# The closing LayerNorm of the last two graphs, block by block on VectorE with separate stores

## Chip, cores and metric

The kernel runs on one core of a Trainium2 chip. The metric is device time in microseconds (us) of one execution, as the median of several. The core's engines work side by side, each through its own instructions in order: TensorE (PE in the profile; PEld is its weight loads), VectorE (DVE), ScalarE (ACT), GpSimd (POOL) and SyncE (SP), which issues the DMA transfers. They wait for each other through semaphores.

## The reference

64 graphs of 256 nodes with 256 features each pass four graph-attention layers. After each layer a residual is added and the rows are normalized without gain or bias:

```python
x = _layernorm(x + _L0_gnn_ref(x, adj, ...), axis=-1)   # 4 heads, projections, own norm
x = _layernorm(x + _L1_gnn_ref(x, adj, ...), axis=-1)   # 8 heads, then a GELU MLP of 1024
x = _layernorm(x + _L2_gnn_ref(x, adj, ...), axis=-1)   # additive attention scores
x = _layernorm(x + _L3_gnn_ref(x, adj, ...), axis=-1)   # scores (x * a_k) @ x.T by edge type
return x
```

`_layernorm` is `(x - m) / sqrt(v + 1e-5)` over the 256 features of a row. For layer 3 the weights are a softmax over the neighbours of a node; only the normalization that follows layer 3, the one that makes the output, is touched here.

## The kernel before

A graph is two blocks (q = 0 and 1) of 128 nodes; a tile `[128, 2, 256]` holds both blocks of a graph, nodes on the 128 partitions. Each graph's work is cut into seven generators named a, u, z, b, w, c and o (`thread_a` to `thread_o`), and each `yield` in them ends a step. Many graphs are in flight together. The order of the steps is written out by hand: `FIRST` lists the steps of the start, `PLACES` gives every step of the middle a due time relative to its graph, and `LAST` lists the steps of the closing stretch, as pairs of a thread's letter and a graph (counted from graph 48 in base 36, so `oe` is a step of `thread_o` of graph 62 and `of` one of graph 63). A small wrapper, `InOrder` (L466), ties each engine's instructions to this order; that is why nearly all rows of the profile carry its line L475, and why groups are told apart by tiles.

`thread_o` (L991) is layer 1's second MLP product, layer 2 and layer 3. Its end goes like this. `values_of` (L974) takes the blocks in the order 1, 0. For each it makes two matmuls into a PSUM tile `pm` (softmax weights times values, and a column with the sum of weights); VectorE takes the reciprocal `r` of that sum and computes `y = pm * r + x` with `scalar_tensor_tensor`, whose accumulator output gives the row sum `sums`. `renormed` (L961) then calls `moments` (L636), in which ScalarE squares the centred rows of both blocks (`xn<-y,sums`, with an accumulator output `sq`), and GpSimd works on two columns at once, one for each block: `ve` from `sq`, `rstd = ve ** -0.5`, and in two instructions `nm = -mean * rstd`. `scaled` (L655) has ScalarE write `xn = y * rstd + nm`, one instruction a block, and SyncE stores both blocks of the graph with one DMA of 256 KB (`out<-xn`). Where no `sums` are handed over, `renormed` uses `stats` (L614) instead, in which VectorE's `bn_stats` and `bn_aggr` make mean and variance `mv`; and `scaled` without `nm` uses VectorE's `tensor_scalar`.

Behind the last step of the plan stand some checks of the input (L1155 to L1171): maxima and sums in `tops`, comparisons `good`, their minimum `all_good`, a matmul over the partitions and the comparison `flag`. They are issued straight to the engines, not through `InOrder`, so that they may be placed anywhere that their data allow. All five engines then load `flag` (L1180) and branch on it (L1181) past a slow general version of the kernel (`any_input`), which the inputs measured here don't need. The rows of L1204 are the closing waits and the barrier of all engines.

Of the kernel before, what the change touches and what calls it, by code (L numbers as in the profile page):

```python
# [8 lines left out]
F32 = mybir.dt.float32  # L9
# [4 lines left out]
ALU = mybir.AluOpType  # L14
AX = mybir.AxisListType

P = 128
N = 256
D = 256
NC = D // P  # L20
G = 2
QB = N // P
TB = G * QB
T = G * N
W = D + 4
DFF = 1024
NF = DFF // P
EPS = 1e-5
# [12 lines left out]
PSR = True  # L41
SQ = True
WARM = 2
XQ = True
DIRECT = {0: ('x', 'z', 'o', 'yT'), 63: ('yT', 'n2', 'n3', 'o')}
BUFS = {'t': 7, 'q': 3, 'k': 1, 'v': 3, 'y': 4, 'z': 4, 'xb': 4, 'both': 2, 'xn': 6, 'mask': 9, 'e': 7, 'x0': 3, 'turned': 2, 'blk': 4, 'oT': 3, 'zs': 1, 'rr': 2, 'xT': 1, 'qT': 1, 'kT': 1, 'adj': 2, 'adjb': 1, 'adjT': 1, 'hT': 2, 'ea': 3}
# [403 lines left out]
def usual_input(ctx: ExitStack, tc: tile.TileContext, a: dict, out: bass.AP, flag: bass.AP):  # L450

    nc = tc.nc
    B = a["x"].shape[0]
# [4 lines left out]
    act = ctx.enter_context(tc.tile_pool(name="act", bufs=1))  # L458
    small = ctx.enter_context(tc.tile_pool(name="small", bufs=8))
# [25 lines left out]
    PE, DVE, ACT, POOL, SP = (InOrder(e) for e in (nc.tensor, nc.vector, nc.scalar, nc.gpsimd, nc.sync))  # L485
    matmul, transpose = PE.matmul, PE.transpose

    def new(pool, shape, dtype, name, bufs=None, tag=None):
        tag = tag or name
        if bufs is None:  # L490
            bufs = BUFS.get(tag)
        t = pool.tile(shape, dtype, name=name, tag=tag, **({} if bufs is None else dict(bufs=bufs)))
        return t
# [3 lines left out]
    warm = new(ps_s, [P, 2, QB * N], F32, "ps", 2)  # L497
    for _ in range(WARM):
        matmul(warm[:, 0, :].rearrange("p (k j) -> p k j", k=4), ones, ones.unsqueeze(1).to_broadcast([P, 4, P]), start=True, stop=True)
    ident = const.tile([P, P], F32, name="ident")  # L500
    make_identity(nc, ident)
    mhalf = const.tile([P, 2 * TB], F32, name="mhalf")
# [11 lines left out]
    r_3 = const.tile([P, B, QB], F32, name="r_3")  # L514
# [6 lines left out]
    def load_x(g):  # L521
        turned = None
        if FX and "x" not in DIRECT.get(g, ()):
            turned = new(io, [P, NC, N // 32, 32], F32, "turned")
            parts = a["x"][g].rearrange("(t i) (c k j) -> k i c t j", i=32, c=NC, j=32)
            for k in range(P // 32):
                if XQ:
                    SP.dma_start(turned[32 * k:32 * k + 32], parts[k])
                for c in range(0 if XQ else NC):
                    SP.dma_start(turned[32 * k:32 * k + 32, c], parts[k, :, c])  # L530
# [83 lines left out]
    def stats(src, twice=False, centre=False):  # L614

        k = 2 if twice else 1
        st = new(small, [P, QB, 6], F32, "st", 8)
        mv = new(small, [P, QB, 2], F32, "mv", 12)
        for q in range(QB):
            DVE.bn_stats(st[:, q, :], src[:, q, 0:D])  # L620
        for q in range(QB):
            DVE.bn_aggr(mv[:, q, :], st[:, q, :])
        ve = new(small, [P, k, QB], F32, f"ve{k}", 8)
        POOL.tensor_scalar(ve[:, 0], mv[:, :, 1], EPS, None, ALU.add)
        if twice:
            POOL.tensor_scalar(ve[:, 1], mv[:, :, 1], 1.0 + EPS, EPS * EPS, ALU.mult, ALU.add)
        rstd = new(small, [P, k, QB], F32, f"rstd{k}", 12)
        POOL.tensor_tensor(rstd, ve, mhalf[:, 0:k * QB].rearrange("p (k t) -> p k t", k=k), ALU.pow)
        nm = None
        if centre:  # L630
            nm = new(small, [P, QB], F32, "nm", 12)
            POOL.tensor_tensor(nm, mv[:, :, 0], rstd[:, k - 1], ALU.mult)
            POOL.tensor_scalar(nm, nm, -1.0, None, ALU.mult)
        return mv, rstd, nm, ve
# [326 lines left out]
    def renormed(y, sums=None):  # L961
        if sums is None:
            mv, rstd, nm, _ = stats(y, centre=SCN)
        xn = new(act, [P, QB, W], F32, "xn")
        POOL.memset(xn[:, :, D:D + 1], 1.0)
        if sums is not None:
            rstd, nm, _ = moments(y, sums, xn)
            mv = None
        yield
        scaled(xn, y, mv, rstd[:, 0], nm)  # L970
        yield
        return xn

    def values_of(e, v, one, x, rs):  # L974
        y = None
        for q in (1, 0):
            po = new(ps_m, [P, one + 1], F32, "pm", 4)
            for kc in range(QB):
                matmul(po, e(kc, q), v[:, kc, 0:one + 1], start=kc == 0, stop=kc == QB - 1)
            yield  # L980
            if y is None:
                y = new(act, [P, QB, D], F32, "y")
                sums = new(small, [P, QB], F32, "sums", 8) if SQ else None
            r = rs[:, q:q + 1]
            DVE.reciprocal(r, po[:, one:one + 1])
            DVE.scalar_tensor_tensor(y[:, q, :], po[:, 0:D], r, x[:, q, 0:D], ALU.mult, ALU.add,
                                     **(dict(accum_out=sums[:, q:q + 1]) if SQ else {}))
            yield
        return y, sums

    def thread_o(g, s):  # L991
        mask = s["mask"]
        hT = s["hT"]
        pm = new(ps_m, [P, QB, D], F32, "pm", 4)
        for q in range(QB):
            for c in range(NF):
                matmul(pm[:, q, :], hT[:, c, q * P:(q + 1) * P], w2[:, c, :], start=c == 0, stop=c == NF - 1)
            yield
        y = s["both"]
        DVE.tensor_tensor(y, pm, y, ALU.add)  # L1000
        yield
        x = yield from renormed(y)

        xT = yield from flipped(x, not FN2, "n2", g)
        yield
        wh = new(act, [P, QB, W], F32, "v")
        pms = []
        for q in range(QB):
            pm = new(ps_m, [P, D + 3], F32, "pm", 4)
            for c in range(NC):  # L1010
                matmul(pm, xT[:, q, c, :], wx[:, c, :], start=c == 0, stop=c == NC - 1)
            pms.append(pm)
        yield
        POOL.memset(wh[:, :, D + 3:D + 4], 1.0)
        for q in range(QB):
            ACT.copy(wh[:, q, 0:D + 3], pms[q])
        ex = new(small, [P, QB, 3], F32, "ex", 4)
        ACT.activation(ex, wh[:, :, D:D + 3], AF.Exp)
        yield
        pt = new(ps_m, [P, N], F32, "pm", 4)  # L1020
        for q in range(QB):
            transpose(pt[:, q * P:(q + 1) * P], ex[:, q, 0:1].to_broadcast([P, P]), ident)
        yield
        e2 = new(act, [P, QB, N], F32, "q")
        for kc in range(QB):
            DVE.tensor_scalar(e2[:, kc, :], pt, ex[:, kc, 1:2], ex[:, kc, 2:3], ALU.mult, ALU.max)
        DVE.tensor_tensor(e2.rearrange("p k q -> p (k q)"), e2.rearrange("p k q -> p (k q)"), mask, ALU.mult)
        yield
        y, sums = yield from values_of(lambda kc, q: e2[:, kc, q * P:(q + 1) * P], wh, D + 3, x, new(small, [P, QB], F32, "r", 8))
        x = yield from renormed(y, sums)  # L1030

        xT = yield from flipped(x, not FN3, "n3", g)
        yield
        xa = new(act, [P, QB, NC, P], F32, "t")
        for c in range(NC):
            ACT.activation(xa[:, :, c, :], xT[:, :, c, :], AF.Identity, scale=a0[:, c:c + 1])
        yield
        ps = new(ps_m, [P, N + P], F32, "pm", 4)
        for kc in range(QB):
            for c in range(NC):  # L1040
                if kc == 0:
                    matmul(ps[:, 0:N].rearrange("p (q j) -> p q j", q=QB), xT[:, 0, c, :], xa[:, :, c, :],
                           start=c == 0, stop=c == NC - 1)
                else:
                    matmul(ps[:, N:N + P], xT[:, 1, c, :], xa[:, 1, c, :], start=c == 0, stop=c == NC - 1)
        yield
        e = new(act, [P, QB * N], F32, "q")
        low = new(act, [P, N + P], F32, "k")
        most = e[:, 0:N + P]
        ACT.activation(most, ps, AF.Exp, bias=shift)  # L1050
        ACT.activation(low, ps, AF.Exp, bias=shift, scale=SLOPE)
        yield
        DVE.tensor_tensor(most, most, low, ALU.max)
        for to, of in ((slice(0, N), slice(0, N)), (slice(N, N + P), slice(N + P, 2 * N))):
            DVE.tensor_tensor(e[:, to], e[:, to], mask[:, of], ALU.mult)
        yield
        pt = new(ps_m, [P, P], F32, "pm", 4)
        transpose(pt, e[:, P:N], ident)
        yield
        ACT.copy(e[:, N + P:2 * N], pt)  # L1060
        yield
        at = ((0, P), (N + P, N))
        y, sums = yield from values_of(lambda kc, q: e[:, at[kc][q]:at[kc][q] + P], x, D, x, r_3[:, g])
        x = yield from renormed(y, sums)
        SP.dma_start(out[g].rearrange("(q p) d -> p q d", p=P), x[:, :, 0:D])
        yield

    def loading():
# [68 lines left out]
    def threads_of(g):  # L1137
        s = {}
        return {"a": thread_a(g, s), "u": thread_u(g, s), "z": thread_z(g, s), "b": thread_b(g, s), "w": thread_w(g, s),
                "c": thread_c(g, s), "o": thread_o(g, s)}  # L1140
# [67 lines left out]
```

## Time and profile before

| what | value |
|---|---|
| median of 3 runs | 2371.16 us (2369.64, 2371.16, 2371.6) |
| profiled execution, its own time | 2374.09 us |
| its span | 2372.3 us |
| TensorE busy | 2338.2 us, 99% |
| VectorE busy | 1924.6 us, 81% |
| ScalarE busy | 1819.8 us, 77% |
| GpSimd busy | 686.9 us, 29% |
| stores of the output | 64 DMAs of 256 KB |
| end of TensorE's last attention product | 2361.43 us |
| end of ScalarE's last scaling | 2366.27 us |
| issue of the last store | 2366.30 us |

The span is the stretch from the first to the last recorded instruction; the execution's own time includes what lies around it. Lines of a timeline give the start in us from the span's start, the length in us, the engine, the source line, the operation, its tiles (out<-in) and how many instructions are merged; a bracket names the idle time before and what ended it. A "q" behind an engine's name stands for its sequencer: waits, branches and DMA issues.

### The profile page before, as it was taken

What the parts mean: (1) busy time and instruction counts of PE and PEld (TensorE: products, weight loads), DVE (VectorE), ACT (ScalarE), POOL (GpSimd) and SP (SyncE); (2) the same over time, 40 slices, a digit from 0 to 9 for tenths busy, and PEclk for the clock granted to TensorE, in tenths of its full rate; (3) what the DMA queues carried; (4) which work ended last, traced back from release to release, by engine and by line L of the source; (5) the groups of instructions that cost most, each with busy time, mean ns of one, the idle gap of its engine ahead of it and who ended that gap; (6) DMA issues with size and microseconds to landing.
All of it is one profiled execution on the core that took longest, in us unless ns stands there. A gap on an engine that the chain in (4) does not pass through costs nothing.

```text
span 2372.3 us, 50135 instructions
## 1 busy us (share of the span) xinstructions
PE 2338.2 (99%) x16124; PEld 1882.1 (79%) x16124; DVE 1924.6 (81%) x6175; ACT 1819.8 (77%) x3976; POOL 686.9 (29%) x1742
## 2 busy tenths in 40 slices
PE   8999999999999999999999999999999999999997
PEld 5677788788788788788788887887887887877786
DVE  5898888888878878878888888888788788778764
ACT  5677877778787788788777777787877887777766
POOL 1122323322332332223223223223323232323232
PEclk9999999999999999999999999999999999999999
DMA  5455555555555555555555555555545545455442
GB/s 129 103 113 118 109 117 112 110 117 116 110 120 111 115 120 112 117 116 110 123 112 107 121 113 111 118 112 112 121 111 116 119 110 120 103 109 116 90 86 68
DMA packets 1088884, 265.08 MB, mean 112 GB/s; under 512 B 859364, under 2 KB 1088232, under 8 KB 1088616
## 3 DMA queue, kind: packets, MB, share of 16 engines
q1 hardware_dynamic: 1088136, 261.42, 51.3%
q8 instruction: 130, 2.13, 0.4%
q14 instruction: 138, 1.13, 0.2%
q10 hardware_dynamic: 416, 0.39, 0.1%
q0 software_dynamic: 64, 0.00, 0.0%
HBM read 153.37 MB, written 99.88 MB: 107 GB/s over the span
## 4 chain that ended last, share of the span: by engine, by line
PE 90%; DMA 3%; ACT 2%; DVE 2%; SPq 2%; issue 1%; POOL 1%; DVEq 0%; ACTq 0%; POOLq 0%
PE pm L475 80%; PE ps L475 10%; SPq L475 2%; DMA blk<-rows 1%; ACT xn L475 1%; DMA rows<-z 1%; DMA turned<-in_x 0%; ACT e L475 0%; DMA adj<-in_adj 0%; DVE y L475 0%; ACT z L475 0%; POOL rstd L475 0%; DMA rr<-lines 0%; DVE e L475 0%; DVE xT L475 0%
## 5 line engine op out<-in xcount | busy, mean ns | idle before, releaser
L475 DVE SCALAR_TENSOR_TENSOR e<-e,mask 128x256 f32<-128x256 f32 x1024 | 368.8, 420 | 210.9 <-ACT e L475 210.8
L475 PE MATMUL pm<-t,L_gnn_W 128*128 128x256 f32 x2048 | 459.7, 382 | 0.4 <-ACT oT L475 0.4
L475 PE MATMUL pm<-L_gnn_W,hT 128*128 128x256 f32 (+1 forms) x2064 | 455.0, 380 | 0.1
L475 PEld LDWEIGHTS pm<-t,L_gnn_W 128*128 128x128 f32 x2048 | 384.5, 190 | 67.4 <-issue 16.1
L475 PEld LDWEIGHTS pm<-L_gnn_W,hT 128*128 128x128 f32 (+1 forms) x2064 | 389.2, 189 | 54.6 <-issue 1.7
L475 ACT ACTIVATE e<-ps 128x1024 f32<-128x1024 f32 x384 | 381.1, 1018 | 51.4 <-PE ps L475 50.7
L475 POOL TENSOR_TENSOR rstd<-ve,mhalf 128x2 f32<-128x2 f32 (+1 forms) x384 | 314.4, 819 | 32.0
L475 POOL TENSOR_SCALAR ve<-sq 128x2 f32<-128x2 f32 x256 | 75.4, 294 | 798.1 <-ACT xn L475 526.8
L475 POOL TENSOR_SCALAR ve<-mv 128x2 f32<-128x2 f32 x192 | 48.1, 251 | 784.5 <-DVE rz L475 462.1
L475 DVE STREAM_TRANSPOSE t<-blk 128x512 f32<-128x512 f32 x313 | 219.6, 704 | 16.7 <-DMA blk<-rows 16.1
L475 ACT ACTIVATE hT<-pm,b 128x256 f32<-128x256 f32 x512 | 201.2, 474 | 17.3 <-PE pm L475 16.5
L475 ACT ACT_TABLE_LOAD x127 | 162.9, 1283 | 2.4 <-PEq L1194 0.7
L475 DVE TENSOR_TENSOR e<-e,mask 128x1024 f32<-128x1024 f32 x128 | 150.9, 1218 | 11.6 <-ACT e L475 11.5
L475 PE MATMUL ps<-t 32*128 32x256 f32 x2048 | 151.1, 404 | 5.2 <-ACT t L475 4.1
L475 ACT ACTIVATE xn<-y,nm,rstd 128x256 f32<-128x256 f32 x256 | 138.5, 593 | 11.0 <-POOL nm L475 9.0
L475 ACT ACTIVATE xn<-y,sums 128x256 f32<-128x256 f32 x256 | 126.6, 497 | 18.2 <-DVE y L475 18.0
L475 PEld LDWEIGHTS ps<-t 32*128 32x128 f32 x2048 | 95.5, 186 | 56.5 <-ACT oT L475 19.7
L475 ACT ACTIVATE few_out<-few 128x8 f32<-128x8 f32 x64 | 13.3, 208 | 162.2 <-DVE few L475 162.1
L475 POOL TENSOR_SCALAR nm<-nm 128x2 f32<-128x2 f32 x320 | 128.9, 403 | 28.0
L475 PE MATMUL pm<-xn,q 128*128 128x257 f32 x512 | 130.9, 381 | 3.5 <-ACT q L475 3.4
L475 DVE SCALAR_TENSOR_TENSOR y<-pm,r,xn 128x256 f32<-128x256 f32 x256 | 123.9, 484 | 9.6
L475 PE MATMUL pm<-e,v 128*32 128x256 f32 x2048 | 124.0, 383 | 5.0 <-DVE e L475 4.6
(149 smaller groups left out, 4646.0 us busy)
## 6 DMA issues: line engine op xcount, KB each, us to landing
blk<-rows SPq DMA_DIRECT2D x1252, 64.0 KB, 2.4
rows<-xn SPq DMA_DIRECT2D x252, 128.0 KB, 2.1
x<-in_x SPq DMA_DIRECT2D x64, 256.0 KB, 3.3
adj<-in_adj SPq DMA_DIRECT2D x64, 256.0 KB, 3.6
rr<-lines SPq DMA_DIRECT2D x128, 128.0 KB, 3.7
out<-xn SPq DMA_DIRECT2D x64, 256.0 KB, 2.5
turned<-in_x SPq DMA_DIRECT2D x252, 64.0 KB, 2.6
rows<-z SPq DMA_DIRECT2D x126, 128.0 KB, 1.9
```

The costliest lines, as they stand in the source:

```text
L475: ins = call(*args, **kw)
```

## The change

A new constant `LATE = 2` selects the last two graphs, 62 and 63. For all others nothing is changed. For these two:

- `values_of` gets a function that it calls as soon as a block's `y` is there, and no longer accumulates `sums`.
- That function takes `bn_stats` and `bn_aggr` of the one block on VectorE, and on GpSimd `ve` and `rstd` of one column.
- After both blocks, VectorE scales them (block 1, then block 0) with `tensor_scalar`, `(y - mean) * rstd`, and each block is stored by a DMA of its own, 128 KB.
- ScalarE's squares and scalings, GpSimd's two `nm` instructions and the memset of a column of ones in `xn` are gone for these graphs. The number of steps of `thread_o` stays, and `LAST` is unchanged.

```diff
+LATE = 2
...
-    def values_of(e, v, one, x, rs):
+    def values_of(e, v, one, x, rs, after=None):
...
-                sums = new(small, [P, QB], F32, "sums", 8) if SQ else None
+                sums = new(small, [P, QB], F32, "sums", 8) if SQ and after is None else None
...
-                                     **(dict(accum_out=sums[:, q:q + 1]) if SQ else {}))
+                                     **({} if sums is None else dict(accum_out=sums[:, q:q + 1])))
+            if after is not None:
+                after(y, q)
             yield
...
-        y, sums = yield from values_of(lambda kc, q: e[:, at[kc][q]:at[kc][q] + P], x, D, x, r_3[:, g])
-        x = yield from renormed(y, sums)
-        SP.dma_start(out[g].rearrange("(q p) d -> p q d", p=P), x[:, :, 0:D])
+        block = lambda kc, q: e[:, at[kc][q]:at[kc][q] + P]
+        if g < B - LATE:
+            y, sums = yield from values_of(block, x, D, x, r_3[:, g])
+            x = yield from renormed(y, sums)
+            SP.dma_start(out[g].rearrange("(q p) d -> p q d", p=P), x[:, :, 0:D])
+            yield
+            return
+        known = {}
+
+        def block_done(y, q):
+            st = new(small, [P, QB, 6], F32, "st", 8)
+            mv = new(small, [P, QB, 2], F32, "mv", 12)
+            DVE.bn_stats(st[:, q, :], y[:, q, 0:D])
+            DVE.bn_aggr(mv[:, q, :], st[:, q, :])
+            ve = new(small, [P, 1, QB], F32, "ve1", 8)
+            POOL.tensor_scalar(ve[:, 0, q:q + 1], mv[:, q, 1:2], EPS, None, ALU.add)
+            rstd = new(small, [P, 1, QB], F32, "rstd1", 12)
+            POOL.tensor_tensor(rstd[:, 0, q:q + 1], ve[:, 0, q:q + 1], mhalf[:, q:q + 1], ALU.pow)
+            known[q] = mv, rstd
+
+        y, _ = yield from values_of(block, x, D, x, r_3[:, g], block_done)
+        xn = new(act, [P, QB, W], F32, "xn")
+        for q in (1, 0):
+            mv, rstd = known[q]
+            DVE.tensor_scalar(xn[:, q, 0:D], y[:, q, :], mv[:, q, 0:1], rstd[:, 0, q:q + 1], ALU.subtract, ALU.mult)
+            SP.dma_start(out[g, q * P:(q + 1) * P, :], xn[:, q, 0:D])
+            yield
         yield
```

## The prediction

> **What bounds the kernel now.** I read the page first, then its chain of work that ended last, then the last 15 us instruction by instruction, because the diff touches only graphs 62 and 63.
>
> ```profile
> span 2372.3 us, 50135 instructions
> ...
> PE 2338.2 (99%) x16124; PEld 1882.1 (79%) x16124; DVE 1924.6 (81%) x6175; ACT 1819.8 (77%) x3976; POOL 686.9 (29%) x1742
> ...
> PE 90%; DMA 3%; ACT 2%; DVE 2%; SPq 2%; issue 1%; POOL 1%; DVEq 0%; ACTq 0%; POOLq 0%
> ```
>
> The reader sees TensorE (PE) busy 99% of the span and carrying 90% of the chain. In the built order of the changed program TensorE's instructions are the same in number and order, and the other engines differ only from the closing steps of graphs 61 to 63 on. So everything before about 2359 us keeps its time, and only the tail can move. Its timeline (start, length, engine, operation):
>
> ```profile
> 2361.68 0.48 DVE L475 SCALAR_TENSOR_TENSOR y<-pm,r,xn 128x256 f32<-128x256 f32 x1
> ...
> 2362.48 0.14 DVE L1165 TENSOR_SCALAR good<-tops 128x1 f32<-128x1 f32 x1
> ...
> 2363.20 3.07 ACT L475 ACTIVATE xn<-y,nm,rstd 128x256 f32<-128x256 f32 x6
> ...
> 2363.42 0.14 DVE L1171 TENSOR_SCALAR flag<-pm 1x1 int32<-1x1 f32 x1 [0.48 <-PE pm L1170]
> ...
> 2364.30 3.02 SPq L475 DMA_DIRECT2D out<-xn  x3
> ```
>
> The last attention sum is ready on VectorE (DVE) at 2362.16, ScalarE (ACT) scales six blocks until 2366.27, and SyncE issues the last store at 2366.30. Yet the span ends at 2372.3: 6 us follow. The other string of work is the flag: VectorE has it at 2363.56, and then every engine branches on it (L1181) and meets in a barrier (L1204). The rows of those two lines (duration min/median/max in ns, first and last start):
>
> ```profile
> L1181 SPq EVENT_SEMAPHORE  x8: 17/17/17, 2368.5 to 2370.3; - x8
> L1181 PEldq COMPARE_BRANCH  x1: 4229/4229/4229, 2364.2 to 2364.2; - x1
> ...
> L1181 ACTq COMPARE_BRANCH  x1: 45/45/45, 2366.0 to 2366.0; - x1
> ```
>
> ```profile
> L1204 ACTq EVENT_SEMAPHORE  x2: 17/17/17, 2371.4 to 2372.3; - x2
> L1204 DVEq EVENT_SEMAPHORE  x2: 21/21/21, 2371.5 to 2372.3; - x2
> ...
> L1204 PEldq EVENT_SEMAPHORE  x2: 51/51/51, 2371.9 to 2372.3; - x2
> ```
>
> TensorE's branch takes 4.23 us where ScalarE's takes 0.05. In the stretch 2364.5 to 2365.5 the DMA view has one 16 KB packet on instruction queue q8 at 10.5% of 16 engines over 1 us, which is 1.7 us; from 2368.5 to 2370 there is another at 4.0% over 1.5 us, 1.0 us. I read them as TensorE's code loads. The barrier opens for ScalarE and VectorE at 2371.4 to 2371.5, for TensorE only at 2371.9, and all leave at 2372.3. So two strings end together: stores landed (SyncE's eight waits, done 2370.3), and **flag to TensorE**: 2363.56 + 8.76 = 2372.3.
>
> **The change part by part.** Call the blocks X1, X0 (graph 62) and Y1, Y0 (graph 63).
>
> *Removed:* on ScalarE eight ACTIVATEs (four squares, four scalings, 0.5 to 0.6 each) and four accumulator reads of 0.19. They end the store string now; what is late next decides.
>
> *VectorE.* The accumulator read (0.08) goes. Each block now is: weighted sum 0.48, bn_stats 0.40 (row mean of st<-y), bn_aggr 0.17, the next reciprocal 0.16, gaps of 0.04 between dependent ones (2334.82 + 0.17 to 2335.02 is one), less 0.05 overlap: 1.28 a block. From the first sum at 2359.27 the blocks start at 2359.27, 2360.55, 2361.83, 2363.11; TensorE, done at 2361.43, is no longer what they wait for. The last bn_aggr ends at 2364.42, with the two L1162/L1163 reductions in its gaps. That is 2.3 later than the last sum ends now.
>
> *GpSimd (POOL)* works in order: X1, X0, then all of graph 61's norm, then Y1, Y0. Rows between 2358 and 2366: ve 0.19, rstd 0.71, nm 0.20 and 0.22, gaps 0.08. The one-column rstd is not in the trace: two columns cost 0.71 and the four-column row averages 1.06, which would give 0.57 on that slope; above I bound it by 0.71. X0 can start at 2361.76 (0.08 behind its bn_aggr) and ends 2362.6 to 2362.75. Graph 61, which starts its ve at 2360.21 today, then needs 0.17 + 1.57 and ends at 2364.35 to 2364.5; its two scalings and its store go 2.5 us later, beside the rest. Y1 and Y0 need 0.80 to 0.99 each: Y0's rstd is there at 2365.95 to 2366.4. The gain of dropping ScalarE's squares is given back in this queue.
>
> *VectorE again.* The four scalings stand in the order X1, Y1, X0, Y0, so X1 starts only behind the last bn_aggr and X0 waits behind Y1 for Y1's rstd, though its own is 2.6 us old. The last scaling starts at 2366.03 to 2366.45. A 128x256 tensor_scalar from SBUF to SBUF is not in the trace: the copy hT<-bv of that size takes 0.28, q<-pm,ex 0.54 from PSUM; I take 0.4. It ends at 2366.3 to 2367.0 against ScalarE's 2366.27. So the store string gains nothing: -0.0 to +0.7 at the last issue.
>
> *Stores:* 256 KB for each graph as before, in two halves; SyncE issues two more (0.37 each, spread over 2 us, hidden behind the waits for scalings). A lone 256 KB store landed after 2.2, the last three after 3.6 to 4.2; a half bounded by 2.2 and 3.6 lands at 2368.6 to 2370.6, against 2369.9 now.
>
> *The flag moves behind the norm.* The checks L1165 to L1171 are not held by the hand-written order; in the built program good, all_good and flag stand on VectorE after the four scalings. Today they take 1.09 us (2362.48 to 2363.56) while VectorE is idle. Now they start 0.07 before the last scaling ends: flag at 2367.35 to 2367.97, **3.8 to 4.4 later**, 4.05 with middle values. Behind it wait TensorE's and VectorE's branches. TensorE's code loads lie on that path; the first took 1.7 us beside three 256 KB stores, the second 1.0 alone. Most stores will have landed by the new first load (about 2369.2), so I take 0.5 off (bounds 0 and 0.7). Sum: 4.05 - 0.5 = **+3.5 us** (bounds +3.1 to +4.4). The span becomes 2375.8.
>
> *A rule that bears on it.* The Trainium skill, "Runtime: NRT & Kernel Launch", section Instruction fetch mechanics, says that a taken branch whose target is not in the loaded window waits for a DMA fetch of the page; TensorE's 4.23 us and the q8 packet agree. "Advanced Engine Details and Errata", section Control Flow Timing, gives a compare-and-branch about 108 ns; ScalarE's 45 ns fits that order of size, TensorE's row does not, and the row decides. By 108 ns the flag string would have 4 us to spare and the sum would be that of the third rival.
>
> The profiled execution took 2374.09, 1.8 beyond its span; the median of the three runs is 2371.16, 2.9 below it. I add the difference to the median: 2371.16 + 3.5 = **2374.7 us**, +0.15%. About 0.2% (4.74 us, beyond 2375.9 or below 2366.4) is what a measurement of this kernel can tell from no change.
>
> **The rivals.**
>
> 1. *GpSimd is held up by VectorE, slower by more than 0.2%.* Over the whole run GpSimd's rows are longer than in the quiet tail: nm 0.40 against 0.20, rstd 0.77 against 0.71, ve 0.25 to 0.29 against 0.19. Today VectorE is mostly idle while GpSimd works in the tail; after the change it runs bn_stats and scalings beside it. At these means the four ve/rstd pairs and two nm after X1 grow by 4 x 0.16 + 2 x 0.19 = 1.0, on top of the upper 4.4, less 0.5: +4.9, 2376.1. It decides from 1.2 us that Y0's rstd comes later than my middle 2366.2. For it: those means. Against it: beside weighted sums in the tail (2361.68 to 2362.16) the rows kept their 0.71 and 0.22.
>
> 2. *TensorE's second load is not waited for.* Then the late 2371.9 is only a slow poll, and the end follows from TensorE's arrival (2368.5 now): 4.05 - 0.5 puts it at 2372.0, SyncE's last waits and the barrier add 1.6: span 2373.6, +1.3, 2372.5. Against it: the packet at 2368.5 to 2370 and the 0.5 us that TensorE alone is late.
>
> 3. *The change does what its words say for the stores, and the flag stays hidden.* TensorE's branch would have to be short, so that only the last landing counts: 2368.6 to 2370.6 instead of 2369.9, middle -0.5: 2370.7. Against it: the 4.23 us row.
>
> **How the numbers follow.** Forecast 58% (own range 2373.5 to 2376.2, its bounds and 0.5 to 1 us for the spread of the runs, 2369.64 to 2371.6; about a tenth of it lies beyond 2375.9). Rival 1 18%, all counted as slower. Rival 2 12%, rival 3 12%, of which 3 points for a gain beyond 0.2% that I can't derive. Slower 0.06 + 0.18 = 0.24, faster 0.03, same 0.73. The range 2371.5 to 2376.6 takes in the forecast, rival 2 and most of rival 1 and leaves out rival 3.
>
> **What would show it.** Right: TensorE's instructions end near 2361.4 as now; Y0's rstd ends near 2366.2 behind a GpSimd queue without idle gaps from 2361.8; the last VectorE scaling ends near 2366.6; flag near 2367.6; TensorE's branch 3.5 to 4.2 long; its barrier row near 2375.4 and later than the other engines'. Wrong: a flag before the scalings, a TensorE branch under 1 us, a barrier that opens for all engines at once, or GpSimd pairs over 1.1 us. If anything before 2359 us moves, the reading that only the tail is touched is wrong.

## The result and the profile after

The kernel after takes **2376.73 us** (median of 11 runs, 2373.96 to 2379.72), the kernel before in 11 runs 2371.16 us (2369.64 to 2374.53). The ratio is 1.0019 with a 95% interval of 1.0011 to 1.0028: slower by 4.5 us, 2.6 to 6.6. The profiled execution of after took 2376.31 us. From its page:

```profile
span 2374.1 us, 50125 instructions
...
PE 2337.2 (98%) x16124; PEld 1879.3 (79%) x16124; DVE 1928.0 (81%) x6183; ACT 1816.4 (77%) x3964; POOL 686.9 (29%) x1740
...
PE 90%; DVE 3%; DMA 2%; ACT 2%; SPq 2%; POOL 1%; issue 1%; DVEq 0%; POOLq 0%; ACTq 0%
```

TensorE has the same 16124 instructions and the same share of the chain. The two profiled spans differ by only 1.8 us, less than the medians (5.6) and the ratio (4.5). The reason lies ahead of the change. In the run of before, TensorE's granted clock was halved for one stretch more, 2352.2 to 2355.6. The same five microseconds in both traces (length; busy time of PE, PEld, DVE, ACT, POOL with counts; granted clock; DMA share; GB/s), first before, then after:

```profile
2350.00:2355.00 5.00, 4.00 (x14) 3.00 (x15) 1.31 (x4) 4.06 (x12) 1.73 (x8) 0.72 0.17 57
```

```profile
2350.00:2355.00 5.00, 4.32 (x22) 3.16 (x22) 1.20 (x5) 4.65 (x12) 1.44 (x6) 1.00 0.17 57
```

At 0.72 TensorE has 14 products in these 5 us, at 1.00 it has 22. A stretch of 3.4 us at half speed loses 1.7 us, and the last attention product indeed ends at 2361.43 before and 2359.76 after. So I compare from that product's end to the end of the span, called the **tail**. It is 10.89 us before and 14.35 after: **+3.46 us**.

VectorE's timeline in the tail of after:

```profile
2361.17 0.48 DVE L476 SCALAR_TENSOR_TENSOR y<-pm,r,xn 128x256 f32<-128x256 f32 x1
...
2361.77 0.42 DVE L476 BATCH_NORM_STATS2 st<-y 128x6 f32<-128x256 f32 x1
...
2362.29 0.17 DVE L476 BATCH_NORM_AGGREGATE mv<-st 128x2 f32<-128x6 f32 x1
2362.37 0.38 DVE L476 TENSOR_SCALAR xn<-y,mv,rstd 128x256 f32<-128x256 f32 x1
2363.51 1.28 DVE L476 TENSOR_SCALAR xn<-y,mv,rstd 128x256 f32<-128x256 f32 x3 [0.75 <-POOL rstd L476]
2364.70 0.15 DVE L1192 TENSOR_SCALAR good<-tops 128x1 f32<-128x1 f32 x1
...
2365.78 0.15 DVE L1198 TENSOR_SCALAR flag<-pm 1x1 int32<-1x1 f32 x1 [0.68 <-PE pm L1197]
```

X1's scaling comes right behind the last `bn_aggr`; before the next three VectorE waits 0.75 us for GpSimd's `rstd` of Y1; `good` starts 0.09 before the last scaling ends, and `flag` stands at 2365.93. That is 6.17 behind the product, where it was 2.13. GpSimd's queue, from X0 over graph 61 to Y1 and Y0:

```profile
2360.24 0.57 POOL L476 TENSOR_TENSOR rstd<-ve,mhalf 128x1 f32<-128x1 f32 x1
...
2361.22 0.71 POOL L476 TENSOR_TENSOR rstd<-ve,mhalf 128x2 f32<-128x2 f32 x1
...
2362.92 0.56 POOL L476 TENSOR_TENSOR rstd<-ve,mhalf 128x1 f32<-128x1 f32 x1
...
2363.75 0.59 POOL L476 TENSOR_TENSOR rstd<-ve,mhalf 128x1 f32<-128x1 f32 x1
```

Then the branch (L1208 in this kernel) and the closing barrier (L1231), durations min/median/max in ns, first and last start:

```profile
L1208 SPq EVENT_SEMAPHORE  x8: 17/17/17, 2367.0 to 2367.6; - x8
L1208 ACTq COMPARE_BRANCH  x1: 45/45/45, 2366.8 to 2366.8; - x1
...
L1208 PEldq COMPARE_BRANCH  x1: 3569/3569/3569, 2366.9 to 2366.9; - x1
```

```profile
L1231 SPq EVENT_SEMAPHORE  x6: 17/28/2281, 2368.0 to 2374.0; - x6
...
L1231 ACTq EVENT_SEMAPHORE  x2: 17/17/17, 2371.4 to 2374.1; - x2
...
L1231 PEldq EVENT_SEMAPHORE  x2: 51/51/51, 2373.7 to 2374.1; - x2
```

The last of SyncE's eight waits at L1208 starts 7.8 us behind the product, where it was 8.9; TensorE's branch still takes 3.57 us. The barrier row of ScalarE comes at 2371.4, TensorE's at 2373.7: TensorE alone is late, by 2.3 us, where it was 0.5. (SyncE's wait of 2281 ns is an earlier one; it ends at 2370.4, when VectorE goes on behind its own branch.) Flag to end is 8.18 us (before: 8.76). The two code loads (transfers of 16 KB on instruction queue q8) start 8.2 and 11.5 us behind the product (before: 3.8 and 8.3).

The stores changed too. Those issued in the tail and their times from issue to landing, before and then after:

```profile
L475 SPq DMA_DIRECT2D out<-xn x3: 372/372/1021, 2364.3 to 2366.3; - x3
...
DMA to landing us min/median/max: 3.6/3.8/4.2
```

```profile
L476 SPq DMA_DIRECT2D out<-xn x5: 350/377/445, 2362.8 to 2365.4; - x5
...
DMA to landing us min/median/max: 1.7/1.8/2.2
```

Landing took half as long. This view's landing is the signal of completion, which for the last store of before comes 0.45 us behind its last data (8.48 and 8.03 behind the product). In the kernels with five stores the signal of the last one isn't recorded, so there the view covers four; one of the four is graph 61's, of 256 KB. The halves of 128 KB seem to explain it; the experiments show that they don't.

### The profile page after: what moved, and what is told of

It reads as the page before. It is cut to its first block, busy times and chain, and to the rows that moved or that the text cites. A ratio compares the mean times of both kernels' runs of the same rounds, so it can differ in the third digit from the quotient of the medians.

```text
span 2374.1 us, 50125 instructions
## 1 busy us (share of the span) xinstructions
PE 2337.2 (98%) x16124; PEld 1879.3 (79%) x16124; DVE 1928.0 (81%) x6183; ACT 1816.4 (77%) x3964; POOL 686.9 (29%) x1740
## 3 DMA queue, kind: packets, MB, share of 16 engines
q8 instruction: 130, 2.13, 0.4%
## 4 chain that ended last, share of the span: by engine, by line
PE 90%; DVE 3%; DMA 2%; ACT 2%; SPq 2%; POOL 1%; issue 1%; DVEq 0%; POOLq 0%; ACTq 0%
PE pm L476 80%; PE ps L476 10%; SPq L476 2%; DVE e L476 1%; DMA blk<-rows 1%; DVE y L476 0%; POOL rstd L476 0%; DMA turned<-in_x 0%; ACT xn L476 0%; ACT e L476 0%; ACT z L476 0%; DMA bk<-in_L_gnn_bk 0%; DMA rr<-lines 0%; DVE st L476 0%; DVE both L476 0%
## 5 line engine op out<-in xcount | busy, mean ns | idle before, releaser
L476 POOL TENSOR_TENSOR rstd<-ve,mhalf 128x2 f32<-128x2 f32 (+2 forms) x386 | 315.3, 817 | 32.2
L476 POOL TENSOR_SCALAR ve<-mv 128x2 f32<-128x2 f32 (+1 forms) x196 | 49.2, 251 | 791.3 <-DVE rz L476 461.7
L476 ACT ACTIVATE hT<-pm,b 128x256 f32<-128x256 f32 x512 | 201.6, 474 | 17.1 <-PE pm L476 16.4
```

What stands on the lines that cost most here:

```text
L476: ins = call(*args, **kw)
```

## The experiments

**My theory:** the loss is the flag's delay, passed on to the end through TensorE's code loads; the norm itself gains nothing. **Rivals:** the norm or its five stores make the tail longer; or GpSimd does. The ratio compares each kernel with runs of before on its own chip; its interval is about 2 us to either side, so it tells only the large steps apart, and each tail is that of one profile. Flag, last scaling, last store issued and landed are in us behind the end of the last attention product; the branch, flag to end and tail are lengths in us; "landed" is the last data of the stores.

| kernel | flag | last scaling | last store issued | landed | TensorE's branch | flag to end | tail | ratio to before (95%) |
|---|---|---|---|---|---|---|---|---|
| before | 2.13 | 4.84 | 4.86 | 8.03 | 4.23 | 8.76 | 10.89 | 1 |
| after | 6.17 | 5.03 | 5.61 | 7.34 | 3.57 | 8.18 | 14.35 | 1.0019 (1.0011 to 1.0028) |
| before_again | 2.13 | 4.83 | 4.86 | 7.67 | 3.97 | 8.13 | 10.26 | 1.0004 (0.9995 to 1.0013) |
| after_again | 6.17 | 5.03 | 5.61 | 7.33 | 3.77 | 8.12 | 14.29 | 1.0019 (1.001 to 1.0028) |
| flag_late | 6.06 | 4.85 | 4.88 | 6.67 | 3.49 | 8.03 | 14.09 | 1.0017 (1.0008 to 1.0026) |
| flag_early | 3.30 | 5.02 | 6.82 | 8.53 | 3.81 | 8.38 | 11.67 | 1.001 (1.0001 to 1.002) |
| no_branch_before | 2.12 | 4.84 | 4.86 | 6.65 | none | 6.11 | 8.24 | 0.9991 (0.9982 to 1.0) |
| no_branch_after | 6.16 | 5.03 | 5.60 | 7.33 | none | 2.6 | 8.76 | 0.9989 (0.998 to 0.9998) |
| flag_62_after | 0.71 | 5.19 | 5.76 | 9.41 | 3.79 | 11.59 | 12.30 | 1.0002 (0.9993 to 1.0011) |
| one_store | 6.09 | 4.96 | 5.42 | 7.77 | 3.77 | 8.78 | 14.87 | 1.0016 (1.0007 to 1.0025) |
| g1_before | 2.13 | 4.84 | 4.86 | 7.36 | 3.59 | 7.81 | 9.94 | 0.9998 (0.9989 to 1.0007) |
| short_before | 2.13 | 5.02 | 5.05 | 8.01 | 0.37 | 8.10 | 10.23 | 1.0001 (0.9992 to 1.001) |
| short_after | 6.17 | 5.03 | 5.61 | 7.33 | 0.37 | 3.34 | 9.51 | 0.9996 (0.9987 to 1.0005) |
| short_flag_late | 6.04 | 4.84 | 4.86 | 6.65 | 0.37 | 2.84 | 8.88 | 0.9992 (0.9983 to 1.0001) |

### Both kernels once more

No edit.

> The kernel before once more, unchanged, against itself. I call 'tail' the time from the end of TensorE's last attention product to the end of the span: 10.9 us in the profile before, 14.4 in the profile after. Flag theory (the end is the flag plus TensorE's branch and its two code loads): the tail stays at 10.9 within 0.5, flag 2.1 behind the product; ratio 1.000 within the noise, and what the span varies by lies ahead of the tail, in how often the clock is halved. If instead the tail itself varies by 2 us or more from one profile to the next, the 3.5 us between the two profiles prove nothing.

> The changed kernel once more. Flag theory: tail 14.4 within 0.5, flag about 6.2 behind the last product, so 3.5 us slower than the kernel before, ratio 1.0015. Rival (something ahead of the tail became slower too, since the medians on record are 5.6 us apart): ratio 1.0024 with the tail still 3.5 longer.

The ratio of after is 1.0019 again (medians 2374.79 beside 2371.53, +3.3 us, where the first pair gave +5.6), and the tail is +4.03 this time, because before's is 0.63 shorter (10.26), a little more than the 0.5 that I had allowed. So +3.5 to +4.0 us of tail stand behind the +4.5.

### The late flag alone, with the old norm

From before; the checks get one comparison more, which reads a result of the last graph's last scaling, so that `flag` can't be earlier:

```diff
+    last = {}
+
     def thread_o(g, s):
...
         x = yield from renormed(y, sums)
+        last["x"] = x
...
-    good = const.tile([P, 7], F32, name="good")
+    good = const.tile([P, 8], F32, name="good")
...
+    nc.vector.tensor_scalar(good[:, 7:8], last["x"][:, 1, 0:1], 1e30, None, ALU.is_lt)
```

> The norm and the stores of the kernel before; the check gets an eighth comparison that reads ScalarE's last scaled block, so that the flag comes behind the last scaling. Flag theory: flag about 3.7 later than before, TensorE's first code load is no longer beside the stores (0.5 less), tail 14.0 to 14.6, time +3.2 us, ratio 1.0013. Rival (VectorE's norm, GpSimd's queue or the split stores make the loss): tail 10.9, ratio 1.000.

Its branch and barrier rows:

```profile
L1185 PEldq COMPARE_BRANCH  x1: 3489/3489/3489, 2364.6 to 2364.6; - x1
```

```profile
L1208 ACTq EVENT_SEMAPHORE  x2: 17/17/17, 2368.8 to 2371.9; - x2
...
L1208 PEldq EVENT_SEMAPHORE  x2: 51/51/51, 2371.6 to 2371.9; - x2
```

The old norm with the flag 3.9 later has nearly the whole loss: tail 14.09, ratio 1.0017. Again TensorE's barrier row is the late one, 2.8 us behind ScalarE's. And a surprise in its stores, which are before's three of 256 KB:

```profile
L475 SPq DMA_DIRECT2D out<-xn x3: 372/372/372, 2360.7 to 2362.7; - x3
...
DMA to landing us min/median/max: 2.1/2.1/2.2
```

They land after 2.1 us, not after 3.6 to 4.2. So it isn't their size that made before's slow.

### The new norm with the flag ahead of the scalings

From after; the checks become a function, whose last VectorE instructions go through `InOrder`:

```diff
         def block_done(y, q):
...
+            if g == B - 1 and q == 0:
+                pm = checks_until_sum()
             DVE.bn_stats(st[:, q, :], y[:, q, 0:D])
             DVE.bn_aggr(mv[:, q, :], st[:, q, :])
+            if g == B - 1 and q == 0:
+                DVE.tensor_scalar(flag, pm[0:1, :], P - 0.5, None, ALU.is_lt)
```

> The norm and the stores of the changed kernel; the checks are put by hand behind the last weighted sum, ahead of the last bn_stats, and the flag ahead of the four scalings. Flag theory: flag 3.6 behind the last product instead of 6.2, tail 11.8 to 12.4, so 2.0 to 2.6 us faster than the changed kernel and 0.9 to 1.5 slower than the kernel before. Rival (the norm itself makes the loss): tail 14.4 as with the change.

The flag comes 2.87 us earlier than in after, and the tail is 2.68 shorter (11.67, just below the expected 11.8 to 12.4): nearly all of it comes through. The ratio falls to 1.001. What remains against before is 0.8 to 1.4 us of tail, about the flag's remaining 1.17.

### No branch at all

From each kernel; the general version is left out:

```diff
-    unusual = nc.values_load(flag)
-    with tc.If(unusual > 0):
-        any_input(tc, a, out)
```

> The kernel before without the load of the flag, the branch and the general version behind it (left out: the fallback for unusual inputs; the flag is still computed). Only the stores and the closing barrier are left at the end. Flag theory: TensorE loads no code across the branch; the last store landed 7.7 to 8.0 us behind TensorE's last product in two profiles of the kernel before, SyncE's waits and the barrier add about 2, so the tail is 9.7 to 10.4, at most 1 us shorter than with the branch (10.3 and 10.9). Rival (the code loads hide behind the stores in the kernel before anyway): the same 10.3 to 10.9.

> The changed kernel without the load of the flag, the branch and the general version (left out: the fallback for unusual inputs). Flag theory: the norm block by block was worth something that the flag hid: the stores landed 7.3 behind the last product in both profiles of the changed kernel, so the tail is 9.2 to 9.6, 0.4 to 0.8 shorter than the kernel before without its branch and 4.5 to 5 shorter than the changed kernel. Rival (GpSimd's queue and the order of the scalings ate the gain): the tail equals that of the kernel before without its branch, or is longer.

Both tails are shorter than expected: before's is 8.24 where I had 9.7 to 10.4, after's 8.76 where I had 9.2 to 9.6. So the branch costs the kernel before 2.0 to 2.7 us, and not at most 1. And the order turns round in the profile. The new norm is 0.52 us longer than the old one when nothing else is in the way, and not shorter, as I had expected here: I had taken before's late landing (8.03) for the old norm's own. Without the branch it lands at 6.65. The two kernels' stores:

```profile
L475 SPq DMA_DIRECT2D out<-xn x3: 372/373/373, 2362.5 to 2364.5; - x3
...
DMA to landing us min/median/max: 2.1/2.1/2.2
```

```profile
L476 SPq DMA_DIRECT2D out<-xn x5: 350/377/442, 2363.3 to 2365.8; - x5
...
DMA to landing us min/median/max: 1.7/1.8/2.2
```

The halves land 0.3 to 0.4 us faster, but the last is issued 0.74 later (5.60 against 4.86): 0.19 for the later scaling and the rest for SyncE, which starts the last issue 0.57 behind the last scaling's end where it was 0.02. SyncE's order is X1, Y1, X0, graph 61, Y0: graph 61's store, whose scalings end in after at 3.90, stands behind X0's and is issued at 5.11 to 5.51, and Y0's has to follow it. The two ratios are too close to order them (0.9991 and 0.9989).

### The flag before all stores

From after; the check leaves out the reciprocals of the last two graphs:

```diff
-    r_all = r_3.rearrange("p g t -> p (g t)")
+    r_all = r_3[:, 0:B - 2, :].rearrange("p g t -> p (g t)")
```

> The changed kernel with its branch, but the check leaves out the reciprocals of graphs 62 and 63, so that the flag doesn't wait for them and stands on VectorE behind the third weighted sum. Flag theory: the flag comes 0.5 to 0.9 behind the last product, its string of about 8.2 ends at 8.7 to 9.1, and the stores set the end: tail 9.5 to 10.0, about 4.5 us faster than the changed kernel and 0.5 to 1 faster than the kernel before (ratio 0.9996 to 0.9998). Rival (a branch costs what it costs wherever it stands): tail 13 or more.

This failed: 12.30, over 2 us longer than the expected 9.5 to 10.0. (The ratio, 1.0002, is too coarse to show it.) The flag is 5.46 us earlier than in after, and TensorE is no longer late (its barrier row comes with ScalarE's). But its two loads, 2.37 and 6.74 behind the product, now fall into the stores. Rows of the branch, then the stores:

```profile
L1208 PEldq COMPARE_BRANCH  x1: 3793/3793/3793, 2361.0 to 2361.0; - x1
...
L1208 DVEq COMPARE_BRANCH  x1: 76/76/76, 2365.3 to 2365.3; - x1
...
L1208 DVEq EVENT_SEMAPHORE  x1: 21/21/21, 2368.7 to 2368.7; - x1
```

```profile
L476 SPq DMA_DIRECT2D out<-xn x5: 350/377/473, 2362.6 to 2365.4; - x5
...
DMA to landing us min/median/max: 1.8/3.0/4.2
```

The last store lands 9.41 behind the product, 2.1 later than in after, 3.65 us behind its own issue. VectorE branches at 2365.3 and goes on only at 2368.7, as in after, where these are 2366.9 and 2370.3.

### One store for both blocks

From after:

```diff
-            SP.dma_start(out[g, q * P:(q + 1) * P, :], xn[:, q, 0:D])
+            if q == 0:
+                SP.dma_start(out[g].rearrange("(q p) d -> p q d", p=P), xn[:, :, 0:D])
```

> The changed kernel with one store of 256 KB for each of the last two graphs, issued behind the second scaling, instead of two of 128 KB; the norm and the flag stay. Flag theory: the stores are not at the end, so nothing changes: tail 14.1 to 14.4, flag 6.2, ratio to the kernel before 1.0015 to 1.0019. Rival (the split stores are part of the loss): the tail is shorter by 0.5 us or more.

Tail 14.87, 0.5 longer than expected, and ratio 1.0016: no gain in the tail, and a ratio 0.0003 lower, far inside the interval. The split stores are no part of the loss. Nor does SyncE's wait go with the two additional issues: the last store is still issued 0.46 us behind its scaling (5.42 against 4.96), again right behind graph 61's.

### A shorter general version

If TensorE's far jump is the bridge from the flag to the end, a shorter jump must break it. `g1_before` takes the general version one graph at a time instead of two; the short kernels also leave layers 0 and 1 out of it. `short_flag_late` puts the late flag on the old norm:

```diff
-G = 2
+G = 1
...
-        x = yield from layer0(x, bias0, s)
-        x = yield from layer1(x, bias1, s)
```

> The kernel before, with the general version behind the branch written for one graph at a time instead of two (same function, half the instructions: TensorE jumps over 274 instead of 482, VectorE over 190 instead of 282). Nothing that is executed changes except the distance of the jump. Code-load theory (TensorE's 4 us branch and its late barrier are loads of code that the jump makes necessary, and loads beside the stores delay these by 1 us or more): at least one of TensorE's two loads goes; with one left the tail is 9.0 to 9.8, with none 8.7 to 9.3, against 10.3 and 10.9; ratio 0.9993 to 0.9996. Rival (a taken branch on TensorE costs 4 us whatever its distance): tail 10.3 to 10.9, branch 4 us.

> The kernel before, with a general version that leaves out layers 0 and 1 (not executed for these inputs), so that TensorE jumps over only 75 instructions. Code-load theory: no load on TensorE, its branch is 0.1 us, stores landed 6.7 behind the last product as in the kernel without a branch, tail 8.7 to 9.3. Rival (the branch costs what it costs): tail 10.3 to 10.9.

> The changed kernel with the same short general version. Code-load theory: the flag still comes 6.2 behind the last product, but TensorE's string behind it shrinks from 8.2 to 1 us; SyncE's load of the flag, its waits and the barrier follow the flag in 3.8 to 4.2 us: tail 9.9 to 10.4, about 4 us faster than the changed kernel, and 1 us slower than the kernel before with the short version. Rival (the branch costs what it costs): tail 14.3.

> The norm and the stores of the kernel before, the short general version (layers 0 and 1 left out of it), and the flag tied behind ScalarE's last scaling as in flag_late. Contention theory (code that is loaded while the stores run delays them by 1 to 2 us; behind a near jump TensorE loads one page too, but doesn't wait for it): the loads come after the stores, these land 6.7 behind the last product instead of 8.0, the flag at 6.1 ends the tail 3.3 later at 9.2 to 9.6, 0.6 to 1.0 shorter than short_before although the flag is 3.9 later; ratio about 0.9996. Rival (the late landing in short_before was something else): tail 10.2 or more.

`g1_before` still shows both loads and a branch of 3.59 us; that part of its expectation failed, though its tail is 0.3 to 1.0 shorter. The short kernels break the bridge. Of short_after, the branch and the barrier:

```profile
L1208 PEldq COMPARE_BRANCH  x1: 369/369/369, 2364.6 to 2364.6; - x1
```

```profile
L1231 ACTq EVENT_SEMAPHORE  x2: 17/17/17, 2366.3 to 2366.9; - x2
...
L1231 PEldq EVENT_SEMAPHORE  x2: 51/51/51, 2366.3 to 2366.9; - x2
```

The same norm, the same flag at 6.17, but a branch of 0.37 us and a barrier that opens for all at once: the tail is 9.51 instead of 14.35 (I had expected 9.9 to 10.4), and the ratio 0.9996.

short_before did not reach its 8.7 to 9.3 us: 10.23. One page is still loaded on q8, 3.88 behind the product for 1.74 us, although no engine is seen to wait for it. It lies beside the stores. short_flag_late was run to test that: there the page is loaded at 7.79, when the stores have landed. Stores of short_before, then of short_flag_late:

```profile
L475 SPq DMA_DIRECT2D out<-xn x3: 372/372/952, 2364.5 to 2366.7; - x3
...
DMA to landing us min/median/max: 3.3/3.9/4.2
```

```profile
L475 SPq DMA_DIRECT2D out<-xn x3: 372/372/373, 2363.8 to 2365.7; - x3
...
DMA to landing us min/median/max: 2.1/2.1/2.2
```

With the flag 3.9 us *later* the tail is 1.35 us *shorter* (8.88 against 10.23; expected were 9.2 to 9.6). The load beside the stores is what costs.

## Why the prediction was right, point by point

The forecast was +3.5 us and 2374.7. The tail grew by 3.46 us (4.03 in the second pair); the ratio gives +4.5, within the 0.2% that I called no change. The median of the first pair lies 2 us above the forecast and 0.13 above the range's upper end, that of the second pair, +3.3 against its own before, is near it. The interval, 2.6 to 6.6 us, holds all of these, and what is left between tail and median is not settled. That +3.46 met +3.5 so closely is in part luck, as the term of -0.5 below shows.

- *Only the tail moves.* Right for the change, but my time for it, a product end near 2361.4, was that of one run. Two runs of before end it at 2361.43 and 2360.48, two of after at 2359.76 and 2358.06. Ahead of it TensorE's granted clock was halved for 20.5 and 17.1 us in before, for 17.1 and 10.2 us in after. Half of 20.5 - 17.1 is the first pair's 1.7 us, but before_again and after, both with 17.1, still lie 0.7 us apart, and that stays open.
- *VectorE, 1.28 us a block.* Right: weighted sums start at 2358.67, 2359.92 and 2361.17, 1.25 apart. (The first sum that I started from stands at 2359.33 in the trace of before, not at 2359.27.) The last `bn_aggr` ends 2.70 behind the product where I had 2.99.
- *GpSimd.* Right, in order and in size: the one-column `rstd`, worked out as 0.57, took 0.56 to 0.59. Y0's ends 4.58 behind the product; I had 4.77 (2366.2). ScalarE's squares are given back here: before, the last `rstd` ended at 3.14.
- *VectorE's scalings.* 0.38 to 0.43 for an assumed 0.4; the last ends at 5.03, inside 4.87 to 5.57, 0.19 later than ScalarE's.
- *The store string, -0.0 to +0.7 at the last issue.* It was +0.75. The step that fell short: I let graph 61's store go "beside the rest" and took SyncE's issues as hidden. Graph 61's stands between X0's and Y0's in SyncE's order, and the last issue waits behind it, in one_store too, which has no additional issue. It cost nothing in the measured pair, since TensorE ends last, and it is most of the new norm's loss where there is no branch.
- *Landing.* It falls where I bounded it (7.34 by the last data; the range was 7.2 to 9.2), but not for my reason: halves land after 1.7 to 1.8 us, below my 2.2, and before's 3.6 to 4.2 came from the code loads.
- *The flag 4.05 later.* 4.04. The term that carries the forecast is shown three ways: flag_late makes the loss without the new norm, flag_early takes most of it back with it, short_after takes it away with norm and flag unchanged.
- *Code loads no longer beside stores, -0.5.* Flag to end fell by 0.58 in the first pair, but by 0.01 in the second (8.13 and 8.12), so a gain for TensorE is not shown: the first load took 1.69 and then 1.16 us in the first pair, but 1.44 and 1.38 in the second; what the loads' move did shorten is the stores.
- *Rivals.* GpSimd's rows stayed near those of the quiet tail (first rival): the two-column `rstd` took 0.71, `nm` 0.20 and 0.24. TensorE's second load is waited for, 2.3 us beyond the others (second). The flag came out of cover (third).

On the Trainium skill, "Runtime: NRT & Kernel Launch", section Instruction fetch mechanics: that a taken branch beyond the loaded pages stalls for a fetch fits the runs, 3.49 to 4.23 us with the whole general version behind the jump against 0.37 with a short one. The 108 ns of "Advanced Engine Details and Errata", section Control Flow Timing, were met by TensorE in neither case.

## What to carry to other kernels

Look at what follows the last store: a check or branch at the end has a string of its own, and instructions that the hand-written order does not hold go wherever a change leaves room for them; here a norm that moved the last store's issue by 0.75 us moved TensorE's jump of 3.6 us back by 4 us. Compare tails from a common event rather than spans, since what lies ahead moved single runs by more than the change: over the 14 profiles here that product ends between 2357.5 and 2363.2. And do not put the late work as early as possible without asking what it then runs beside: of the kernels with the new norm and the far jump, flag_early has its flag at 3.30 and a tail of 11.67, flag_62_after at 0.71 and 12.30.

No kernel with a branch beats before beyond its interval: the lowest, short_flag_late, is at 0.9992 (0.9983 to 1.0001) and has only a part of the general version. Of the two without one, no_branch_after is below 1 with its whole interval (0.9989, 0.998 to 0.9998), but it leaves out the fallback for unusual inputs.

## What the runs showed of the hardware

**Code loads beside stores delay the stores**, also when no engine waits for the code. The last store took, from issue to its last data, 3.17 and 2.81 us in the two runs of before, 2.96 in short_before, 2.50 in g1_before and 3.65 in flag_62_after, all with q8 loads in the same microseconds; it took 1.72 to 1.79 in after, after_again, flag_late, short_after, short_flag_late and the two kernels without a branch, where the loads come later or not at all. In one_store it took 2.35 without a load, with three stores of 256 KB issued within 1 us; in flag_early, whose last store is issued late, 1.71, while the three before it took 3.2 to 3.4 to the signal, beside a load. Kernels with stores of 256 KB are on both sides, with the old and the new flag. The packets fit one or two engines that are held up: in short_before the DMA engines are busy for 0.93 of 16 engines' time from 2368.3 to 2369.0, but for 0.07, about one engine's worth, from 2369.1 to 2369.6, with the last store still under way; in flag_62_after it is 0.09 over the last 1.8 us of the stores. That it is an engine that took a packet of code, 16 KB in 0.9 to 1.7 us, is argued: the trace doesn't tell the engine of a packet.

**A far jump costs at the end twice.** Flag to end was 8.0 to 8.8 us in the runs in which TensorE arrived 2 us or more after the others (after, after_again, flag_late, one_store): 0.6 to 1.3 us to the branch, 3.5 to 3.8 us in it, and a second load behind it for which the barrier waits. The first load starts 1.0 to 1.1 us behind TensorE's branch in all twelve profiles with a branch, wherever it stands; the two without one show no such load at the end.
